# One core, cross-attention and soft mixture of experts: the first group's dispatch split into single batches

## The chip, the cores and the metric

The kernel runs on one core of a Trainium2 chip. A core has a matrix engine (PE), whose results go to the accumulator memory PSUM; a vector engine (DVE); a scalar engine for activation functions and copies (ACT); a general engine (POOL); and a queue that issues most transfers (SP). Each engine works through its own list of instructions in the order of the program, and semaphores make one engine wait for another. A matmul has two records: the load of the stationary 128 x 128 operand (PEld) and the pass of the moving columns over it (PE). Both are float32 here, and the trace has two passes for each matmul of the program. The metric is the device time of one execution in microseconds (us); a lower time is better.

## The reference, cut to what matters

There are 16 batches of 100 tokens with 256 features. Each batch attends to its own 361 context rows with 16 heads; then a soft mixture of 16 experts with 64 slots each runs on the normalized result.

```python
x = x + attention(layernorm(x), ctx_1024, ...)          # 16 heads of 16
z = layernorm(layernorm(x)) * norm_g + norm_b           # (b, n, d)
logits = einsum('bnd,esd->bnes', z, se)                 # 1024 slots
dispatch = softmax(logits, axis=tokens)
combine = softmax(logits, axis=slots)
slots = einsum('bnd,bnes->besd', z, dispatch)
gate = gelu(slots @ Wg + bg);  up = slots @ Wu + bu
eout = (gate * up) @ Wd + bd
x = x + einsum('bns,bso->bno', combine, eout)
```

The dispatch of a batch turns its 100 normalized tokens into 1024 slot vectors. Each expert needs its 64 slots of every batch of a group before it can start on that group.

## The kernel before, in words

**Groups and streams.** The batches go in five groups of 2, 2, 4, 4 and 4 (`GROUPS`). For each group there is a stream of attention units (`units`, four units to a batch, each with `maxima`, `queries`, `exponentials` and `values`), and then the dispatch in quarters of 256 slots (`dispatch_quarter`, four experts to a quarter) for each pair of batches. One stream, `all_experts`, runs the experts group by group: `gp` and `up` are the two first products (lines 1265 to 1281), `dn` the product with `Wd` (line 1225), `po` the combination (line 1147). While one group's experts run, the next group's attention is worked in between.

**The planner.** No engine order is written out by hand. At build time, `Clock` keeps a modelled time of each engine, every generator (`Task`) yields the earliest time of its next step, the PSUM banks that it takes and a triple of costs for PE, DVE and ACT, and the loop at the end of the kernel picks the next step. Before the first expert has run (`begun` is false), the steps that something waits for come first (`lead`: the units of the first group; after these `out_work`, the first entry of `dispatches` and `all_experts`). Another step is taken only if its modelled PE, DVE and ACT ends come no later than the next lead step's start plus a slack of 0.15 plus 0.6 of the step's PE cost. If nothing fits, PE gets a `warm_up` matmul on a constant (line 1319), which computes nothing that is used. After `begun`, units and dispatches go first, then side work from `fill` in the order of that list, and the experts fill what is left. While the first group's units run, the side work is sorted by a list of kinds.

**Around the change.** `out_work(b)` closes the attention of batch b: four divisions by the softmax sums on DVE (lines 699 to 707), the projection `o_ps` (line 712), the residual (line 720), the norm (lines 436 to 447), the normalized tokens `xn` (line 733), their transpose `xn_t` (line 738) and the scaled transpose `xnT` (line 744), with which `out_t[b]` is set. A quarter of the first group's dispatch then takes: the logits `lg` of both batches (line 928; 4 matmuls, 8 records, of 200 moving columns each), their maximum over tokens on DVE (line 953), four exponentials with sums on ACT (line 958), a copy of the logits to `lg_all` (line 949), the division on DVE (lines 980 and 983), four transposes `d_t` (line 1006), their copy `disp` (line 1011), the slots `sl` of each batch (line 1018), and the scaled slots, by DVE for the first batch (line 1030) and by ACT for the second (line 1033). At last the running maximum over slots, `top`, is kept up (lines 1050 to 1054), from which `combine_weights` starts. `slots_left[g, q]` counts how many parts of a quarter are outstanding; the experts of quarter q are gated on it.

Side work that can stand in the gaps before the first expert is `later_queries(2)` (`x_t` and `q_ps` of batches 2 and 3), `later_keys(2)` and `later_keys(3)` (context transposes `c_t`, keys `k_ps` on line 609, values `v_ps` on line 659).

**Queues.** SP issues the weights, the context rows (lines 199 to 213), the inputs and, for each batch's keys, four small copies of the mask row from `mrow_d` into `kT` (line 649). All of these share one queue in program order.

## Time and profile before

| | |
|---|---|
| median of 3 executions | 1183.79 us (1183.12 to 1184.21) |
| the profiled execution | 1184.91 us, its span 1183.0 us |
| PE busy | 1160.9 us, 98% of the span |
| ACT, DVE, POOL busy | 547.2, 632.9, 151.3 us |
| warm-up matmuls, line 1319 | 96 records from 1.4 to 78.7 us, 50 of them between 64 and 82 us |
| first expert matmul | 82.1 us |
| mean granted PE clock | 0.996 |

A span is the time from the first to the last recorded instruction; the execution's own time is about 2 us longer. "Busy" of PE counts warm-up matmuls too, so PE at 98% says nothing about how much of the first 82 us is of use. The timeline view gives the start, the length, the engine, the line and the tiles of merged instructions, and in brackets the idle time before them and who ended it.

### The profile page before, as it was taken

The numbers are of one execution on the slowest core, as the hardware profiler recorded it, in microseconds if no ns is written. First come the engines' busy times: TensorE is split into PE (matmuls) and PEld (weight loads), VectorE is DVE, ScalarE is ACT, GpSimd is POOL, SyncE is SP. The second block draws the span as 40 slices with busy tenths as digits, with TensorE's granted clock in tenths as the row PEclk, the third lists the DMA queues.
The fourth block names the chain that finished last, engine by engine and source line by source line (L and its number), as shares of the span: only waits on it lengthen the run. The fifth ranks groups of instructions, "written<-read, shape, count | busy, mean of one in ns | idle before, by whom it ended". The sixth has DMA issues, their size and how long they took to land.

```text
span 1183.0 us, 24384 instructions
## 1 busy us (share of the span) xinstructions
PE 1160.9 (98%) x9815; PEld 899.8 (76%) x9815; DVE 632.9 (53%) x1555; ACT 547.2 (46%) x1120; POOL 151.3 (13%) x255
## 2 busy tenths in 40 slices
PE   8899999999999999999999999999999999999998
PEld 6587878678788777667767777787878878777876
DVE  5755555475544566555386776656533455432222
ACT  3557554466454568444543745536312336314110
POOL 3110301013000043200010100024000003002000
PEclk9999999899999999999999999999999999999999
DMA  5413657345566613223341421333344343344441
GB/s 133 136 37 104 228 172 216 89 126 160 157 224 220 184 17 90 81 50 110 112 105 39 124 77 38 112 126 112 112 142 151 118 147 126 111 133 161 135 129 55
DMA packets 138675, 144.86 MB, mean 122 GB/s; under 512 B 45136, under 2 KB 97314, under 8 KB 138562
## 3 DMA queue, kind: packets, MB, share of 16 engines
q1 hardware_dynamic: 137742, 141.88, 39.5%
q8 instruction: 78, 1.28, 0.5%
q0 software_dynamic: 496, 1.12, 0.3%
q10 hardware_dynamic: 324, 0.29, 0.1%
q14 instruction: 35, 0.29, 0.1%
HBM read 141.60 MB, written 1.66 MB: 121 GB/s over the span
## 4 chain that ended last, share of the span: by engine, by line
PE 95%; DMA 2%; DVE 1%; SPq 1%; ACT 1%; issue 0%; DVEq 0%; ACTq 0%
PE dn L1225 19%; PE gp L1265 19%; PE up L1265 19%; PE sl L1018 5%; PE po L1147 5%; PE at L796 5%; PE at L771 4%; PE lg L928 4%; PE k_ps L609 3%; PE v_ps L659 3%; PE cx L819 3%; PE o_ps L712 1%; PE at L1319 1%; PE q_ps L538 1%; DMA kT<-mrow_d 1%; DVE mxp L776 1%
## 5 line engine op out<-in xcount | busy, mean ns | idle before, releaser
L1265 PE MATMUL gp<-ring,w_all 128*128 128x256 f32 (+1 forms) x1280 | 248.3, 341 | 1.5 <-ACT lg_all L949 1.3
L1265 PE MATMUL up<-ring,w_all 128*128 128x256 f32 (+1 forms) x1280 | 246.8, 340 | 0.0
L1281 DVE SCALAR_TENSOR_TENSOR hT<-up,parT,ge 128x256 f32<-128x256 f32 (+1 forms) x320 | 119.4, 423 | 225.0 <-PE up L1265 163.0
L1225 PE MATMUL dn<-w_all,hT 128*64 128x256 f32 x2048 | 232.8, 382 | 0.0
L1276 ACT ACTIVATE ge<-gp,parT 128x256 f32<-128x256 f32 (+1 forms) x320 | 117.2, 430 | 244.6 <-PE gp L1265 240.5
L1265 PEld LDWEIGHTS gp<-ring,w_all 128*128 128x128 f32 x1280 | 203.0, 191 | 28.5 <-issue 5.5
L1265 PEld LDWEIGHTS up<-ring,w_all 128*128 128x128 f32 x1280 | 203.5, 191 | 21.6 <-issue 1.7
L1225 PEld LDWEIGHTS dn<-w_all,hT 128*64 128x64 f32 x2048 | 143.8, 137 | 77.2 <-issue 10.1
L776 DVE TENSOR_REDUCE mxp<-at 100x4 f32<-100x1444 f32 x64 | 106.2, 1660 | 40.7 <-PE at L771 40.2
L1234 DVE TENSOR_TENSOR ring<-dn,bd_bc 128x512 f32<-128x512 f32 x64 | 44.3, 692 | 139.2 <-PE dn L1225 139.0
L804 ACT ACTIVATE aT<-at 121x1200 f32<-121x1200 f32 x64 | 74.9, 1171 | 55.2 <-PE at L796 49.5
L1276 ACT ACT_TABLE_LOAD x62 | 79.5, 1283 | 33.6 <-PE gp L1265 32.8
L998 DVE STREAM_TRANSPOSE disp<-d_ex 32x128 f32<-32x128 f32 x256 | 77.3, 302 | 4.6
L703 POOL TENSOR_TENSOR cxs<-cxs,rs 128x100 f32<-128x100 f32 x63 | 25.0, 398 | 410.4 <-DVE rs L700 328.6
L1033 ACT ACTIVATE ring<-sl,parT 128x256 f32<-128x256 f32 x64 | 32.7, 562 | 69.4 <-PE sl L1018 67.1
L1018 PE MATMUL sl<-disp,xn 100*128 100x256 f32 x256 | 62.6, 386 | 0.0
L1147 PE MATMUL po<-ring,lg_all 128*100 128x256 f32 x256 | 60.6, 383 | 0.2 <-DVE ring L1234 0.2
L983 POOL TENSOR_TENSOR d_ex<-d_ex,d_sm 128x400 f32<-128x400 f32 x28 | 23.9, 855 | 270.8 <-DVE d_sm L980 269.6
L796 PEld LDWEIGHTS at<-q,kT 32*121 32x121 f32 x1344 | 40.6, 180 | 19.9 <-issue 9.1
L771 PE MATMUL at<-kT,qp 32*100 32x361 f32 x448 | 49.2, 508 | 5.9 <-DMA kT<-mrow_d 5.9
L1018 PEld LDWEIGHTS sl<-disp,xn 100*128 100x128 f32 x256 | 46.6, 190 | 9.4 <-issue 2.8
L804 ACT ACT_TABLE_LOAD x35 | 44.9, 1283 | 18.4 <-PE at L796 10.3
(152 smaller groups left out, 1276.4 us busy)
## 6 DMA issues: line engine op xcount, KB each, us to landing
w_all<-in_L_ffn_Wg_dram SPq DMA_DIRECT2D x80, 512.0 KB
w_all<-in_L_ffn_Wu_dram SPq DMA_DIRECT2D x80, 512.0 KB
w_all<-in_L_ffn_Wd_dram SPq DMA_DIRECT2D x80, 512.0 KB
bd_bc<-in_L_ffn_bd_dram SPq DMA_DIRECT2D x80, 64.0 KB
c_sb<-in_ctx_dram SPq DMA_DIRECT2D x96, 44.0 KB
out_dram<-acc SPq DMA_DIRECT2D x8, 200.0 KB
acc<-in_x_dram SPq DMA_DIRECT2D x7, 200.0 KB
ring<-n_L_ffn_slot_embeds_dram POOLq DMA_DIRECT2D x1, 1024.0 KB, 7.2
```

What stands on the lines that cost most here:

```text
L771: nc.tensor.matmul(self.at[:N, r, :S2], lhsT=self.q[rows], rhs=self.k[rows], start=True, stop=True)
L776: nc.vector.tensor_reduce(mxv[:, :, m : m + 1], self.at[:N, :, :S2], AX.X, ALU.max, negate=True)
L796: nc.tensor.matmul(self.at[: KC + 1, r, c * N : (c + 1) * N], lhsT=self.k[rows, c * KC : c * KC + KC + 1], rhs=self.q2[rows], start=True, ...
L804: nc.scalar.activation(self.aT[: KC + 1], self.at[: KC + 1, :, : 3 * N], AF.Exp)
L928: nc.tensor.matmul(lg[:, c * 2 * N : (c + 1) * 2 * N], lhsT=seT[:, kd, (2 * q + c) * P : (2 * q + c + 1) * P], rhs=xnTs[g][:, kd, b0 * N : ...
L998: nc.vector.transpose(dst[toks, :, :, a, :], src[32 * a : 32 * a + 32, :, :, toks])
L1018: nc.tensor.matmul(sl[:, kd * 256 : (kd + 1) * 256], lhsT=xns[g][:, b0 + i, kd * P : (kd + 1) * P], rhs=disp[:, i, :], start=True, stop=True,)
L1147: nc.tensor.matmul(pos[i][:N, :D], lhsT=lg_all[:, slot, 2 * c + i, :], rhs=eouts_of(g, q)[:, c, 2 * p + i, :], start=c == 0, stop=c == 1,)
L1225: nc.tensor.matmul(dn[S * x : S * x + S, i * D : (i + 1) * D], lhsT=hts[x][fc // FB][0].rearrange("p (f b s) -> p f b s", f=FB, s=S)[:, fc ...
L1265: nc.tensor.matmul(ps[:, f * T : (f + 1) * T], lhsT=w[:, kd, fc * P : (fc + 1) * P], rhs=slots_of(g, q)[:, j, kd].rearrange("p b s -> p (b ...
L1276: nc.scalar.activation(ge[:, cols], ps[:, cols], AF.Gelu, bias=col(8, e, fc))
L1281: nc.vector.scalar_tensor_tensor(out=hT[:, cols], in0=ps[:, cols], scalar=col(NPAR, e, fc), in1=ge[:, cols], op0=ALU.add, op1=ALU.mult,)
```

## The change

The first group (batches 0 and 1) no longer goes through `dispatch_quarter`. A new generator, `dispatch_half(q, i)`, does one quarter for one batch: 100 moving columns in `lg`, two exponentials, two transposes, the slots of one batch with one half scaled on DVE and the other on ACT, and the running maximum of that batch. Batch 0's four quarters run one after the other in a new side task, `early_dispatch`, whose kind stands ahead of `key_work` in the sorted list and which is appended to `fill` ahead of `later_queries` and `later_keys`. Batch 1's four go into `dispatches`, where the four `dispatch_quarter` tasks stood. The counters `left` and `slots_left` of group 0 count batches in place of pairs. The other groups are as before.

```diff
+    half_slots, top_begun = {}, [False, False]
+    def dispatch_half(q, i):
+        def gate():
+            if i not in out_t or (q not in half_slots and not lg_free):
+                return NEVER
+            return max(seT_t[q // 2], out_t[i])
+        yield gate, 1, (0.9, 0.35, 0.75)
+        lg = mm_tile("lg")
+        for c in range(2):
+            for kd in range(KD):
+                nc.tensor.matmul(
+                    lg[:, c * N : (c + 1) * N],
+                    lhsT=seT[:, kd, (2 * q + c) * P : (2 * q + c + 1) * P],
+                    rhs=xnTs[0][:, kd, i * N : (i + 1) * N],
...
+        lgs = lg_all[:, half_slots[q]].rearrange("p (c i) n -> p i c n", i=2)[:, i]
...
+        ex = exs[:, :2, :N]
+        nc.vector.tensor_reduce(mx[:, :2], lgv, AX.X, ALU.max, negate=True)
+        for c in range(2):
+            nc.scalar.activation(ex[:, c], lgv[:, c], AF.Exp,
...
+        nc.scalar.copy(lgs, lgv)
...
+        yield t, 0, (0.0, 0.5, 0.0)
+        nc.vector.reciprocal(sm[:, :2], sm[:, :2])
+        nc.vector.tensor_tensor(ex, ex, sm[:, :2].unsqueeze(2).to_broadcast([P, 2, N]), ALU.mult)
+        yield t, 1, (0.25, 0.0, 0.4)
...
+        for c in range(2):
+            nc.tensor.transpose(tp[:N, c * P : (c + 1) * P], ex[:, c, :], ident)
+        nc.scalar.copy(disp, tp[:N, :256])
+        yield t, 1, (0.87, 0.4, 0.4)
+        sl = mm_tile("sl")
+        for kd in range(KD):
+            nc.tensor.matmul(
+                sl[:, kd * 256 : (kd + 1) * 256],
+                lhsT=xns[0][:, i, kd * P : (kd + 1) * P],
+                rhs=disp,
...
+            if kd == 0:
+                nc.vector.tensor_scalar(dst, srcv, ng_c[kd], nb_c[kd], ALU.mult, ALU.add)
+            else:
+                nc.scalar.activation(dst, srcv, AF.Identity, bias=nb_c[kd], scale=ng_c[kd])
...
+        slots_left[0, q] -= 1
+        left[0] -= 1
+        yield tl, 0, (0.0, 0.4, 0.0)
+        dst = top[0][:, i]
+        if not top_begun[i]:
+            nc.vector.tensor_tensor(dst, lgs[:, 0], lgs[:, 1], ALU.max)
+        else:
+            for c in range(2):
+                nc.vector.tensor_tensor(dst, dst, lgs[:, c], ALU.max)
+        top[1] += 0.5
+    def early_dispatch():
+        for q in range(NQ):
+            yield from dispatch_half(q, 0)
...
-    left = [n // 2 * NQ for n in GROUPS]
-    slots_left = {(g, q): n // 2 for g, n in enumerate(GROUPS) for q in range(NQ)}
+    left = [(n // 2 if g else n) * NQ for g, n in enumerate(GROUPS)]
+    slots_left = {(g, q): n // 2 if g else n for g, n in enumerate(GROUPS) for q in range(NQ)}
...
                     fill.append(Task(slot_work(), ck))
+                    fill.append(Task(early_dispatch(), ck))
                     load_x(1)
...
                     "out_work",
+                    "early_dispatch",
                     "key_work",
...
-                                dispatches.append(Task(dispatch_quarter(g, p, q), ck, 2))
+                                if g == 0:
+                                    dispatches.append(Task(dispatch_half(q, 1), ck, 2))
+                                else:
+                                    dispatches.append(Task(dispatch_quarter(g, p, q), ck, 2))
```

More of the change, by code (lines that the diff above doesn't have):

```diff
@@ L1057, in dispatch_quarter @@
         logits[g, p, q] = slot
+    half_slots, top_begun = {}, [False, False]
[12 more added lines that the diff above has]
+                    rhs=xnTs[0][:, kd, i * N : (i + 1) * N],
+                    start=kd == 0,
+                    stop=kd == KD - 1,
+                )
+        t = ck.run("PE", 0.85, ck.bank())
+        lgv = lg[:, : 2 * N].rearrange("p (c n) -> p c n", n=N)
+        if q not in half_slots:
+            half_slots[q] = lg_free.pop(0)
+            logits[0, 0, q] = half_slots[q]
+        lgs = lg_all[:, half_slots[q]].rearrange("p (c i) n -> p i c n", i=2)[:, i]
+        mx = two.tile([P, 4], F32, tag="mx", name="d_mx")
+        sm = two.tile([P, 4], F32, tag="sm", name="d_sm")
+        if len(exps) < 2:
+            exps.append(const.tile([P, 4, P], F32, name=f"d_ex{len(exps)}"))
+            nc.gpsimd.memset(exps[-1][:, :, N:], 0.0)
+        exs = exps[turn[0] % 2]
+        turn[0] += 1
+        ex = exs[:, :2, :N]
+        nc.vector.tensor_reduce(mx[:, :2], lgv, AX.X, ALU.max, negate=True)
+        t = ck.run("DVE", 0.35, t)
+        for c in range(2):
+            nc.scalar.activation(
+                ex[:, c],
+                lgv[:, c],
+                AF.Exp,
+                bias=mx[:, c : c + 1],
+                accum_out=sm[:, c : c + 1],
+            )
+            t = ck.act("exp", 130, t)
+        nc.scalar.copy(lgs, lgv)
+        tl = ck.copy(200, 0.0)
+        ck.free(tl)
+        yield t, 0, (0.0, 0.5, 0.0)
+        nc.vector.reciprocal(sm[:, :2], sm[:, :2])
+        ck.run("DVE", 0.1, t)
+        nc.vector.tensor_tensor(ex, ex, sm[:, :2].unsqueeze(2).to_broadcast([P, 2, N]), ALU.mult)
+        t = ck.run("DVE", 0.35)
+        yield t, 1, (0.25, 0.0, 0.4)
+        disp_sb = two.tile([P, 2, 256], F32, tag="disp", name="disp")
+        disp = disp_sb[:N, 0]
+        tp = mm_tile("d_t")
+        for c in range(2):
+            nc.tensor.transpose(tp[:N, c * P : (c + 1) * P], ex[:, c, :], ident)
+        nc.scalar.copy(disp, tp[:N, :256])
+        t = ck.copy(256, ck.run("PE", 0.25, t, ck.bank()))
+        ck.free(t)
+        yield t, 1, (0.87, 0.4, 0.4)
[5 more added lines that the diff above has]
+                rhs=disp,
+                start=True,
+                stop=True,
+            )
+        t = ck.pe(512, t, ck.bank())
+        ts = []
+        for kd in range(KD):
+            dst = slots_of(0, q)[:, :, kd, i, :]
+            srcv = sl[:, kd * 256 : (kd + 1) * 256].rearrange("p (e s) -> p e s", s=S)
+            if kd == 0:
+                nc.vector.tensor_scalar(dst, srcv, ng_c[kd], nb_c[kd], ALU.mult, ALU.add)
+                ts.append(ck.psum_dve(256, t))
+            else:
+                nc.scalar.activation(dst, srcv, AF.Identity, bias=nb_c[kd], scale=ng_c[kd])
+                ts.append(ck.copy(256, t))
+        ck.free(max(ts))
+        slot_t[0, q] = max(slot_t.get((0, q), 0.0), *ts)
+        slots_left[0, q] -= 1
+        left[0] -= 1
+        yield tl, 0, (0.0, 0.4, 0.0)
+        if (0, 0) not in tops:
+            tops[0, 0] = [two.tile([P, 2, N], F32, tag="top", name="top"), 0, 0.0]
+        top = tops[0, 0]
+        dst = top[0][:, i]
+        if not top_begun[i]:
+            nc.vector.tensor_tensor(dst, lgs[:, 0], lgs[:, 1], ALU.max)
+            top_begun[i] = True
+        else:
+            for c in range(2):
+                nc.vector.tensor_tensor(dst, dst, lgs[:, c], ALU.max)
+        top[2] = ck.run("DVE", 0.4, tl)
+        top[1] += 0.5
```

## The prediction

> **What bounds the kernel now.** I read the engine slices first, then busy time in windows.

> ```profile
> PE   8899999999999999999999999999999999999998
> 60.00:70.00 10.00, 9.48 (x95) 7.42 (x95) 7.58 (x25) 3.65 (x7) 1.45 (x4) 1.00 0.20 51
> 70.00:80.00 10.00, 9.99 (x68) 8.93 (x67) 4.71 (x13) 5.03 (x16) 2.68 (x5) 1.00 0.01 3
> 80.00:90.00 10.00, 9.02 (x65) 8.66 (x63) 3.56 (x8) 8.01 (x26) 0.00 (x0) 1.00 0.21 58
> ```

> PE is the bound from the first expert matmul (82.1 us) to the end; almost every window after 130 us is full. PE work added after 82 us therefore costs its length, and work moved from there into idle time before 82 us gains its length. Between 64 and 82 us PE looks full but is not: 50 of its records are warm-ups. At the chain's spacing (12 in 1.34 us, so 0.112 us each) that is 5.6 us without use.

> **When does the early half become possible?** This decides most. The timeline:

> ```profile
> 61.27 0.89 PE L796 MATMUL at<-q,kT 32*121 32x100 f32 x24 [0.35 <-DVE q L787]
> 63.77 0.72 PE L819 MATMUL cx<-aT,vpad 120*32 120x100 f32 x24
> 64.86 0.76 ACT L744 ACTIVATE xnT<-xn_t,parT 128x100 f32<-128x100 f32 x2
> 66.12 1.50 PE L1319 MATMUL at<-ident 128*128 128x128 f32 x12
> 68.77 1.38 PE L609 MATMUL k_ps<-cT,wk 128*128 128x361 f32 x4
> 69.98 1.89 PE L659 MATMUL v_ps<-wv,cT 128*121 128x256 f32 x8
> 72.96 1.52 PE L928 MATMUL lg<-xnT,seT 128*128 128x200 f32 x8
> 74.31 2.62 PE L1319 MATMUL at<-ident 128*128 128x128 f32 x22
> 78.95 1.99 PE L1018 MATMUL sl<-disp,xn 100*128 100x256 f32 x8
> ```

> The second batch's last unit is over at 63.77 (`cx`), and the first batch's `xnT` lands at 65.6. Its `out_work` has been low-priority DVE work since 44 us. So batch 0's quarters do not run during the second batch's units; there is nothing to dispatch until they are over. What remains is 65.6 to 73.0 us, while batch 1 goes through `out_work`, and the gaps of its first quarter up to 82 us. No lead step moves ahead of 64 us: the new task has no step ready, and key work of batch 1 stays within the eight side tasks that the planner looks at.

> **Part 1, PE work added.** `lg` had 8 records of 200 columns per quarter and gets 2 x 8 of 100 columns, each with its own load of 128 x 128. The chain of waits has both forms:

> ```profile
> 22.73 1.06 PE q_ps L538 x8
> 80.95 1.37 PE lg L928 x8
> ```

> Eight records of 100 columns take 1.06 us here, 0.97 from the first record to the next product (22.66 to 23.63), and 0.87 in another place (9.66). A halved column count thus does not halve the time; the load sets it. Per quarter 2 x 0.97 - 1.37 = 0.57 us; with the warm-up's load spacing, 2 x 8 x 0.112 - 1.37 = 0.42. Over four quarters +1.7 to +2.3, taken +2.0 us. `d_t` and `sl` keep their number and form.

> [...] The trace has 171 and 121 ns. [...] I use the row, +2.0.

> **Part 2, what the gaps take.** In `fill`, early dispatch stands ahead of the later queries and keys, so where a PE gap is long enough for one step it takes it from them. The k_ps at 68.77 (1.22 us by the chain) is where the first early `lg` goes: the planner sees some 1.9 us to the next lead step, and the step's triple (0.9, 0.35, 0.75) fits. Once its maxima and exponentials are on DVE and ACT, the key steps' own ACT cost no longer fits, so the gap's rest stays warm-up. I followed the planner's rule by hand with its costs and the trace's order:

> - lg, d_t and sl of quarter 0, batch 0 get in before the first expert, little more. Quarters 1 to 3 of batch 0 follow one another serially and must wait.
> - Displaced past the first expert: one k_ps (1.22), three v_ps (1.73 + 0.88), the x_t of batches 2 and 3 (about 0.5): 4.3 us.
> - Warm-ups stay at about 24 calls against 25: the chain of single steps that causes them is still there.

> **Part 3, the chain to the first expert gets shorter.** From `xnT` (73.04) to `gp` (82.14) it is 9.1 us. Batch 1 alone: lg -0.40; maximum over 200 and not 400 elements, 0.58 to about 0.36 (the 200-wide `top` takes 0.35): -0.22; two exponentials of 0.35 in place of four: -0.70; division -0.25; two transposes fewer -0.2; `disp` 0.59 to 0.37 (the 256-wide v_ps copy): -0.22; four sl records fewer -0.86; scaled slots split over DVE and ACT, one each: about -0.5; the next `lg` -0.40. Sum -3.8; the planner's own costs give -4.3. I take the first expert at 78 us, 4.0 earlier.

> **Part 4, after the first expert.** Dispatch work left on PE by then: before, 2.3 (rest of quarter 1) + 2 x 3.7 = 9.7 us; after, half of quarter 1 without its lg (1.2) and five whole halves of about 2.13 (0.97 + 0.3 + 0.86) = 11.8 us, +2.1. With the displaced 4.3 and the 4.0 gained: **+2.4 us** on PE.

> ACT is the other side. Exponential and gelu alternate here:

> ```profile
> 84.77 1.28 ACT L1276 ACT_TABLE_LOAD   x1
> 87.22 1.28 ACT L958 ACT_TABLE_LOAD   x1
> ```

> PE already waits once at 90.36 for PSUM that ACT frees late (1.35 us, the idle in window 80 to 90). Five half batches remain where two quarters did, so I expect one or two more pairs of loads (2.6 us each), and a half's fixed parts cost ACT about 0.25 us a quarter more (copies 2 x 0.3 + 2 x 0.37 against 0.50 + 0.59, two slot evictions unchanged). ACT was busy 22.7 of the 30 us from 80 to 110; plus 3 to 6 it is nearly full. [...] here ACT ended a copy at 84.74 and loaded at 84.77, so 1.28 stands. [...] Bounds of the PE stall: -1.35 (the stall there goes) to +4; nearest row is the one stall of 1.35, so I take **+0.9**.

> Three halves can be in flight over two `d_ex` buffers, so an exponential may wait for the transposes of the half two turns before. Queued behind it on ACT are gelu and the PSUM copies; cover is that those transposes are 0.3 us and picked first. Zero to +1, taken 0. DVE gets about 0.8 us more per quarter and is busy 36 to 78% of these windows: nothing. POOL's clearing of `d_ex` (0.32) only comes earlier, in idle POOL time. The change issues no DMA; the displaced keys' mask copies go out later, needed by batch 3's units after 110 us: nothing.

> **Sum.** +2.4 + 0.9 = +3.3 us on a span of 1183.0, so an execution of about 1188.2 against the profiled 1184.91. That one lay 1.1 us above the median; from 1183.79 the forecast is **1187 us**.

> **A lever that I cannot size.** The order after 82 us changes, and one stall later is large:

> ```profile
> 204.76 2.30 SPq L649 DMA_DIRECT2D kT<-mrow_d  x4
> 209.91 1.54 PE L771 MATMUL at<-kT,qp 32*100 32x361 f32 x8 [5.20 <-DMA kT<-mrow_d]
> 206.00:208.00 2.00, 0.00 (x0) 0.00 (x0) 0.00 (x0) 0.00 (x0) 0.00 (x0) 0.95 1.04 363
> 208.00:210.00 2.00, 0.09 (x4) 0.12 (x4) 0.00 (x0) 0.00 (x0) 0.00 (x0) 0.50 0.55 128
> ```

> Group 2's first unit waits for mask rows that SP could only issue behind batch 5's context loads and two weights. PE's granted clock falls to 0.50 and is 0.54 from 210 to 215. The stall costs 5.2 us and the slow clock some 2.5 to 3. Key work, context loads and unit follow each other as before, so I expect the stall to stay; but if the planner puts one more expert half (1.8 to 3.7 us) in front of the unit, or one less, it moves by that much.

> **Rivals.**
> - *The gaps are filled* (0.13). The 5.6 us of warm-ups take the early halves without displacing keys, and the 1.35 us stall goes: -5.6 - 1.35 + 2.0 = -5, 1179 us. For: 24 records' worth of gap lies in 74 to 82, where three early halves would fit by length. Against: each step must also fit by ACT, which the lead half holds. It decides if two or more whole early halves come before the first expert.
> - *Shorter stall at 205* (0.12). One more expert step before group 2's first unit: up to -7 with the clock fall gone, netting about 1180. Nothing in the profile favours it over its opposite.
> - *Longer stall there, or ACT the bound after 78 us* (0.25): +3 to +8 on top, 1190 to 1195.
> - *A wash* (0.12): the earlier first expert pays for displaced work and for half the loads, 1183 to 1185.
> - The forecast, *displaced, not hidden* (0.38): 1185.5 to 1189.

> **How the numbers follow.** About 0.2% (2.4 us) is what can be told from no change. Faster: most of the first two, 0.21. Same: the wash and the forecast's lower edge, 0.16. Slower: 0.63. Range 1179 to 1196: it takes in both lower rivals' centres and the longer stall; beyond lie about 0.2.

> **What would show it.** Right: `lg` of group 0 has 64 records near 0.12 us spacing; the first sits after 65 us; first `gp` near 78; k_ps, v_ps of batch 3 after it; warm-up records about 94 in all; a stall near 200 with a clock fall. Wrong: warm-ups down to 70 or fewer, an `lg` before 63 us, a first `gp` after 81, more than 2 us of new PE idle between 78 and 110, or a stall near 200 that is gone.

## The result, and the profile after

The changed kernel takes **1187.78 us** (median of 6 executions, 1187.06 to 1190.05); the kernel before took 1184.0 us beside it (6 executions, 1183.12 to 1185.81). The ratio is 1.0034, 95% interval 1.0021 to 1.0047: slower by about a third of a per cent. The profiled execution took 1187.36 us with a span of 1185.6 us, against 1184.91 and 1183.0.

First the engine slices and the windows of the changed kernel (in the windows: the stretch, its length, the busy time and number of instructions of PE, PE's weight loads, DVE, ACT and POOL, the granted clock, the DMA share, GB/s).

```profile
PE   8899999999999899999999999999999999999998
60.00:70.00 10.00, 9.64 (x104) 8.22 (x105) 7.56 (x25) 3.79 (x8) 1.82 (x4) 1.00 0.17 49
70.00:80.00 10.00, 9.57 (x73) 8.71 (x72) 4.08 (x13) 5.93 (x22) 0.33 (x3) 1.00 0.01 2
80.00:90.00 10.00, 8.18 (x50) 6.40 (x50) 6.60 (x18) 7.59 (x25) 1.97 (x2) 1.00 0.19 54
```

The third window is the one to look at: PE is busy 8.18 us where it was busy 9.02. PE's idle time here has grown from 0.98 to 1.82 us, and ACT, which the prediction suspected, is busy 7.59 and was busy 8.01. In the slices of the whole span a dip has appeared too, the 8 in the fourteenth slice, at about 400 us.

The timeline of the changed kernel, cut to what answers the prediction:

```profile
63.39 0.72 PE L819 MATMUL cx<-aT,vpad 120*32 120x100 f32 x24
68.39 1.03 PE L1073 MATMUL lg<-xnT,seT 128*128 128x100 f32 x8
69.26 1.75 PE L1425 MATMUL at<-ident 128*128 128x128 f32 x14
...
77.73 2.36 PE L1371 MATMUL gp<-ring,w_all 128*128 128x128 f32 x16
81.88 1.48 PE L609 MATMUL k_ps<-cT,wk 128*128 128x361 f32 x4
84.17 1.13 PE L659 MATMUL v_ps<-wv,cT 128*121 128x256 f32 x4 [0.81 <-ACT lg_all L1105]
85.36 1.27 POOL L563 TENSOR_TENSOR acc<-acc,bo_bc 100x512 f32<-100x512 f32 x1 [0.85 <-DVE d_sm L1109]
85.39 1.46 DVE L1111 TENSOR_TENSOR d_ex<-d_ex,d_sm 128x200 f32<-128x200 f32 x1
87.00 0.40 PE L1118 MATMUL d_t<-ident,d_ex 128*100 128x128 f32 x2 [0.84 <-DVE d_ex L1111]
```

The second batch's units end at 63.39 and the first early `lg` comes at 68.39. Nothing of batch 0's dispatch lies beside those units. The first expert is at 77.73, 4.4 us earlier by the trace's own time, 4.0 if both traces are set to the first `xn_t` of batch 0 (64.4 and 64.0 us). The `k_ps` and `v_ps` that used to stand at 68.77 and 69.98 now stand behind it. Warm-ups are 94 records, before 96.

The stall at 205 us is gone. The plan now has an expert's `dn`, the `q_ps` and eight `k_ps` records between the issue of the mask rows and the unit that needs them, which starts 9.3 us after that issue (before, it started 5.2 us after it, and PE was idle all that time):

```profile
207.00 2.31 SPq L649 DMA_DIRECT2D kT<-mrow_d  x4
208.74 3.67 PE L1331 MATMUL dn<-w_all,hT 128*64 128x256 f32 x32
216.32 0.87 PE L771 MATMUL at<-kT,qp 32*100 32x361 f32 x8
```

In its place stands a stall near 400 us. Windows of the changed kernel around both places, and its timeline at the second:

```profile
206.00:208.00 2.00, 2.00 (x11) 1.66 (x10) 0.00 (x0) 1.24 (x4) 0.00 (x0) 1.00 0.32 50
400.00:402.00 2.00, 0.00 (x0) 0.00 (x0) 1.93 (x6) 0.33 (x2) 0.70 (x1) 1.00 0.01 5
404.00:406.00 2.00, 2.00 (x8) 1.58 (x7) 1.28 (x3) 0.59 (x1) 0.00 (x1) 0.50 0.33 94
```

```profile
400.18 0.87 DVE L1264 SCALAR_TENSOR_TENSOR acc<-po,c_sm,acc 100x256 f32<-100x256 f32 x2
...
400.96 0.91 DVE L594 STREAM_TRANSPOSE cT<-c_sb 128x704 f32<-128x704 f32 x1
401.90 0.25 DVE L595 STREAM_TRANSPOSE cT<-c_sb 128x64 f32<-128x64 f32 x1
402.07 0.14 DVE L980 RECIPROCAL d_sm<-d_sm 128x4 f32<-128x4 f32 x1
...
402.30 1.68 PE L609 MATMUL k_ps<-cT,wk 128*128 128x361 f32 x4 [3.66 <-DVE d_sm L980]
```

PE stands still for 3.66 us for `k_ps`. The list names `d_sm`, which ended last, but what `k_ps` reads is `cT`, transposed on DVE until 402.15 behind a row of norm and residual work. In the kernel before the same stretch looks like this:

```profile
395.92 3.67 PE L1225 MATMUL dn<-w_all,hT 128*64 128x256 f32 x32
```

There one expert's `dn` stood between the same `lg` and the DVE list, and covered it. The plan of the changed kernel has that `dn` at 389.26, ahead of the `lg`.

Where the time went, counted on PE from the first `xn_t` to the last `dn` (1109.8 us before, 1111.7 after):

| part | us |
|---|---|
| `lg` records, their spacing summed, first `xn_t` to group 2 | 22.5 to 24.2, +1.7 |
| PE idle, 64 to 110 us | 1.35 to 2.43, +1.1 |
| waits too short to show as idle, the same stretch (record spacing over the usual one of its kind) | about +0.4 |
| stall at 205 us with its half clock (6.8 us) gone | -6.6 |
| stall at 402 us with its half clock (3.4 us) new | +6.1 |
| idle between 443 and 778 us | 1.80 to 1.13, -0.7 |

That is +2.0 for a measured +1.9. The two rows of the stalls are sums of record spacing over the usual one and can be off by about half a microsecond. Two places check the table, because both kernels have done the same work on PE there but for the 32 added `lg` records and two warm-ups. At the 145th `gp` record (159 us) the changed kernel is 3.8 us behind, counted from `xn_t`; at the 513th (443 us) it is 2.65 behind. After 406 us the order of PE's records is the same in both.

The profiled pair differs by 2.45 us and the medians by 3.8, so the table explains the traces and not the whole of the medians' difference. Outside this stretch the traces of all kernels here scatter: the first `xn_t` comes between 64.0 and 73.6 us (52.4 in the run that moves the tokens forward), and 8.4 to 9.8 us pass from the start of the last `dn` to the end. So distances from the first `xn_t` to the last `dn` are given below beside the medians.

### The profile page after: what moved, and what is told of

It reads as the page before. It is cut to its first block, busy times and chain, and to the rows that moved or that the text cites. A ratio compares the mean times of both kernels' runs of the same rounds, so it can differ in the third digit from the quotient of the medians.

```text
span 1185.6 us, 24470 instructions
## 1 busy us (share of the span) xinstructions
PE 1163.6 (98%) x9845; PEld 901.5 (76%) x9845; DVE 635.7 (54%) x1572; ACT 551.4 (47%) x1132; POOL 151.3 (13%) x255
## 3 DMA queue, kind: packets, MB, share of 16 engines
q8 instruction: 78, 1.28, 0.5%
## 4 chain that ended last, share of the span: by engine, by line
PE 94%; DVE 2%; issue 1%; ACT 1%; DMA 1%; POOL 0%; SPq 0%; DVEq 0%; ACTq 0%; POOLq 0%
PE dn L1331 19%; PE up L1371 19%; PE gp L1371 19%; PE po L1253 5%; PE at L796 4%; PE sl L1018 4%; PE at L771 4%; PE k_ps L609 3%; PE lg L928 3%; PE cx L819 3%; PE v_ps L659 3%; PE o_ps L712 1%; PE q_ps L538 1%; DVE mxp L776 1%; PE at L785 1%
## 5 line engine op out<-in xcount | busy, mean ns | idle before, releaser
L1033 ACT ACTIVATE ring<-sl,parT 128x256 f32<-128x256 f32 x56 | 28.6, 561 | 59.9 <-PE sl L1018 59.9
L1018 PE MATMUL sl<-disp,xn 100*128 100x256 f32 x224 | 55.0, 388 | 0.7 <-ACT disp L1011 0.7
L796 PEld LDWEIGHTS at<-q,kT 32*121 32x121 f32 x1344 | 40.6, 180 | 19.1 <-issue 8.2
L796 PE MATMUL at<-q,kT 32*121 32x100 f32 x1344 | 49.9, 277 | 3.4 <-DVE q L787 3.3
L700 DVE RECIPROCAL rs<-rs 128x100 f32<-128x100 f32 x64 | 49.8, 778 | 2.2
```

Of the source, the lines that this page charges most:

```text
L700: nc.vector.reciprocal(rs, rs)
L796: nc.tensor.matmul(self.at[: KC + 1, r, c * N : (c + 1) * N], lhsT=self.k[rows, c * KC : c * KC + KC + 1], rhs=self.q2[rows], start=True, ...
L1018: nc.tensor.matmul(sl[:, kd * 256 : (kd + 1) * 256], lhsT=xns[g][:, b0 + i, kd * P : (kd + 1) * P], rhs=disp[:, i, :], start=True, stop=True,)
```

## Experiments

Two things were open: which part of the change costs (the loads, the early task, or merely another plan), and whether the stalls at 205 and 402 us belong to the change or are an accident of the plan.

**The doubled loads alone.** In the kernel before, the first group's `lg` is cut in two halves of 100 columns; costs and plan stay as they are.

```diff
+        parts = 1 if g else 2
+        w = 2 * N // parts
         for c in range(2):
-            for kd in range(KD):
+            for h in range(parts):
+                for kd in range(KD):
...
```

> The kernel before, with each 200-column logits matmul of the first group cut into two of 100 columns; the plan and the order of all else are unchanged. Theory (the load of the stationary operand sets the time of a 100-column record): the 64 records take about 0.11 to 0.12 us each where 32 took 0.17, so +1.4 to +2.3 us, about 1185.9 beside 1184.0, and the first expert matmul about 0.8 us later. Rival (moving columns alone set the time): no change, within 0.5 us.

Measured: 1185.33 us against 1185.07 beside it, ratio 1.0005 (0.9995 to 1.0016). From `xn_t` to the last `dn` 1110.7, +0.9; the `lg` records themselves take 1.7 to 1.8 us more and the first expert is 0.8 us later. So the doubled records are real work on PE: 100 columns don't take half of 200. In the trace before, eight 128 x 128 loads took 1.40 us beside 200 columns (72.77 us), and 0.97 beside 100 (22.66 us) as beside 128 (warm-ups, 20.23 us). With PE's order unchanged, 1.25 us of them are left at 101 us, and a shorter wait between 600 and 650 us takes off another 0.5. The total was less than expected, and its interval includes no change.

**Single batches, all from the list of dispatches.** Both batches go through `dispatch_half`, and there is no side task.

```diff
-                    fill.append(Task(early_dispatch(), ck))
...
                                 if g == 0:
+                                    dispatches.append(Task(dispatch_half(q, 0), ck, 2))
                                     dispatches.append(Task(dispatch_half(q, 1), ck, 2))
```

> The changed kernel without its early task: both batches of the first group go singly through the list of dispatches, after the second batch's tokens are ready. Theory (the early halves only displaced key and value work): the keys and values of batch 3 go back in front of the first expert, the first expert matmul comes at 79 to 82 us, and at the 128th gate record after it (about 119 us) the kernel stands within 1.5 us of the changed one; total 1185 to 1189. Rival (the early halves fill idle time): 3 us or more behind the changed kernel at that place, total above 1190.

Measured: 1186.3 us, ratio 1.0006 (0.9995 to 1.0016); `xn_t` to the last `dn` 1110.2, +0.4. The edit does not do what was expected of it: batch 0 does not wait for batch 1's tokens. The first entry of `dispatches` is a lead step, and of the tokens its gate asks for batch 0's alone. So two `lg` of batch 0 stand ahead of batch 1's `xn_t`, the last line here:

```profile
66.48 0.39 PE L738 MATMUL xn_t<-ident,xn 100*128 100x100 f32 x2
67.40 1.23 PE L1073 MATMUL lg<-xnT,seT 128*128 128x100 f32 x8
...
73.54 1.03 PE L1073 MATMUL lg<-xnT,seT 128*128 128x100 f32 x8
...
75.36 0.39 PE L738 MATMUL xn_t<-ident,xn 100*128 100x100 f32 x2
```

The first comes 0.9 us after the first `xn_t`; in the changed kernel it was 4.3. This run, and the two below that have the same edit, thus compare batch 0 in the lead with batch 0 in the side list, not a late dispatch with an early one. Batch 1's tokens pay for it: their `xn_t` comes 8.9 us after the first, where it was 7.4 before and 6.8 with the change.

The first expert comes 16.6 us after `xn_t` (17.7 before, 13.7 with the change), with 86 warm-ups. From 171 us on PE's order is the one of the kernel before; there the run is 1.7 us behind, and shorter waits later leave 0.4 (the stall at 205 us is there again, now 4.5 us, with a half clock of 6.8 us). The side list thus brings 2.9 us of the earlier first expert, and the end of the kernel does not see it: the change is 1.5 us behind this run by the trace, and about 3.3 by the ratios.

**The early task behind the keys.** `early_dispatch` is appended to `fill` after `later_keys(3)`.

```diff
-                    fill.append(Task(early_dispatch(), ck))
                     load_x(1)
...
                     fill.append(Task(later_keys(3), ck))
+                    fill.append(Task(early_dispatch(), ck))
```

> The changed kernel with the early task put behind the later queries and keys in the side list. Theory (one gap step is traded for another): k_ps and v_ps come back before the first expert, the early logits move behind them, the first expert matmul comes at 80 to 84 us, and warm-ups stay at 85 to 100 records; total within 2 us of the changed kernel unless a later stall moves. Rival (the order of the side list is what costs): warm-ups fall below 75 records and the total falls by 3 us or more against the changed kernel, to 1184 or less.

Measured: 1191.46 us, ratio 1.0063 (1.0042 to 1.0084); `xn_t` to the last `dn` 1115.8. The first expert does not come at 80 to 84 us but here:

```profile
L1371 PE MATMUL gp<-ring,w_all x77: 275/275/377, 100.8 to 130.0; 128*128 128x128 f32 x77
```

(The tile view: count, shortest, median and longest ns, first and last start.) Warm-ups go up to 170 records, 126 of them after 60 us. The idea that keys would fill the gaps first and batch 0 come just after was wrong. Once batch 1's dispatch is a lead step, a task at the end of the list starves: four `lg` start from 72.8 to 88.2 us, after batch 1's tokens, and a fifth at 94.5, just before the first expert, which needs both batches. The gaps are then filled with matmuls that compute nothing. The end of the list is no place for the early task.

**Batch 0's tokens earlier.** In the list of kinds, `out_work` goes ahead of `slot_work` (which prepares the slot vectors that `lg` needs).

```diff
-                    "slot_work",
                     "out_work",
+                    "slot_work",
                     "early_dispatch",
```

> The changed kernel with out_work ahead of the parameter and slot work in the sorted list of side work, so that the first batch's tokens are ready before the second batch's last unit. Theory (DVE has no room for both before the units end: whichever comes second, tokens or slot vectors, keeps the logits late): xnT of batch 0 lands near 50 to 54 us, seT only at 65 to 70 us, the first logits matmul still not before 63 us, total 1186 to 1192. Rival (only the order kept the early halves out of the units): first logits before 60 us, warm-ups down to 75 records or fewer, first expert matmul before 76 us and a total of 1182 to 1185.

Measured: 1190.75 us, ratio 1.0044 (1.0029 to 1.0059). The first `xn_t` comes at 52.4 us, 11.6 us earlier, yet the slot vectors `seT` land only at 70.3 us, the first `lg` is at 71.4, the first expert at 97.6, and there are 148 warm-ups. As expected, whichever of the two inputs of `lg` is second keeps it after the units. In neither order does an early half stand beside the second batch's units.

**The stall at 205 us: mask rows first.** In the kernel before, from batch 4 on the context loads of the next batch go out behind the mask rows of this one. The same edit in the changed kernel, and in the kernel with single batches.

```diff
-        if b + 1 < B and b + 1 not in loads:
+        if b < 4 and b + 1 < B and b + 1 not in loads:
             load_kv(b + 1)
...
+        if b >= 4 and b + 1 < B and b + 1 not in loads:
+            load_kv(b + 1)
```

> The kernel before, with the next batch's context load issued on SP after the mask rows of this batch's keys instead of before them (batches 4 and later). Theory (SP's order makes the stall at 205 us): the 5.2 us wait for the mask rows goes, and with it the 6.8 us at half clock, which costs 3.4: up to -8.6, total 1176 to 1179. Rival (the rows land late because the transfer engines are busy, or another input of the same unit is as late): less than 2 us is gained.

> The changed kernel with the mask rows of the keys issued on SP ahead of the next context load, as in e4. Theory (the changed kernel has lost the stall at 205 us already, and its own stall near 399 us comes from DVE's list, not from SP): little is gained by the queue itself, total 1183 to 1188, behind e4 by 3 us or more. Rival (both stalls come from SP's order): the stall near 399 us goes as well, total 1179 to 1182, level with e4 but for the 1 to 2 us of doubled loads.

> e2 (both batches singly, none early) with the mask rows first, as in e4. Theory (doubled loads cost 1 to 2 us, the early task costs another 2 to 3): 1181 to 1183 where e4 had 1180.1, and 2 us or more ahead of e5. Rival (the loads are hidden and the early task costs nothing; stalls make all of the difference): within 0.7 us of e4, or level with e5.

Measured: before 1180.12 us, ratio 0.9956 (0.9944 to 0.9967), 1104.8 us from `xn_t` to the last `dn`, no stall over 1.4 us and no half clock at 205. With the change 1192.17, ratio 1.0052 (1.0037 to 1.0067), 1114.7, above both expectations, with a wait of 3.66 us before a `k_ps` at 405.8 us and one of 2.04 at 431.6. With single batches 1183.17, ratio 0.9981 (0.9974 to 0.9989), 1106.0. So the old form does have 5 us to gain at 205 (8.6 were thought possible), from the order of the queue alone. Single batches, again with batch 0 in the lead, cost 1.7 us in this plan by 170 us, where PE's order becomes the same, and 1.2 at the end (`lg` +1.9, warm-ups -0.65), close to what the loads are worth; by the ratios it is 3. The change itself landed on the worse side: it never had the stall at 205, and the edit left it its other one. Which of the later waits make up its further 3 us is open.

**A plan without either stall.** The planner's own assumption of how long after its issue a mask row can be used, `MASK_DMA`, goes from 5 to 9 and to 12 us. In the trace before, the first `kT` copies of these keys (line 630) ended at 197.79 us and the unit that needs their mask rows began at 209.91, 12.1 us later. The edit adds no work that is used. It changes the order, and with it what depends on the order: warm-ups (96 become 112 and 158 in the kernel before, 94 become 86 and 124 in the changed one), some ACT table loads, and which engine makes some copies.

```diff
-MASK_DMA = 5.0
+MASK_DMA = 9.0
```

> The kernel before with the planner's allowance for the mask rows' landing at 9 us in place of 5; nothing else is edited, but the plan after the first group moves. Theory (the 205 us stall is the planner's 5 us against some 12 us on the chip): group 2's first unit stands some 4 us later in PE's list, 4 of the 5.2 us of stall and the half clock after it go: 1177 to 1181. Rival (the stall moves with the plan): 1183 or more.

> The changed kernel with the same allowance of 9 us. Theory (the change costs 1 to 2 us of doubled loads and about 3 us by the early task, and has no mask stall to lose): 1184 to 1191, 3 us or more behind the kernel before with 9 us. Rival (the change costs its loads alone): 1 to 2.3 us behind it.

> The kernel before with an allowance of 12 us. Theory: no mask stall and no half clock at 205 us, 1176 to 1182; a unit that waits longer in the plan can cost elsewhere. Rival: 1183 or more.

> The changed kernel with an allowance of 12 us. Theory: 3 us or more behind the kernel before with 12 us, unless a stall of its own plan comes or goes; the first expert matmul stays 3 to 5 us ahead of that kernel's. Rival: 1 to 2.3 us behind it.

| planned distance | before, us | changed, us | `xn_t` to last `dn` | medians' difference |
|---|---|---|---|---|
| 5 us (as given) | 1184.0 | 1187.78 | 1109.8, 1111.7 | +3.8 |
| 9 us | 1177.46, ratio 0.9946 (0.9926 to 0.9966) | 1181.27, 0.9983 (0.9974 to 0.9991) | 1100.9, 1104.6 | +3.8 |
| 12 us | 1189.63, 1.005 (1.0035 to 1.0065) | 1192.4, 1.007 (1.0053 to 1.0086) | 1106.8, 1108.1 | +2.8 |

(Ratios are against the kernel before at 5 us. At 9 us the intervals of the two forms lie apart; at 12 us they overlap.) With 12 us the kernel *before* has the stall that looked like the change's own. From the list of waits of that run:

```profile
PE k_ps L609 <- DVE d_sm L980: 3.7, 1, 3.7
```

It is the same 3.7 us before a `k_ps`, at 405 us, and a fall of the clock follows, 6.8 us long. So this stall belongs to a plan in which no expert's `dn` stands there, not to the change.

At 9 us neither kernel has a stall over 1.5 us after 66 us, nor a half clock before its end, and the change costs 3.8 us by medians and 3.7 by the trace. This pair is clean of the two large stalls. The waits of PE from 60 to 300 us, first before, then changed (total, times, longest):

```profile
PE at L771 <- DMA kT<-mrow_d: 1.1, 1, 1.1
```

```profile
PE k_ps L609 <- DVE cT L595: 1.4, 1, 1.4
PE d_t L1118 <- ACT d_ex L1097: 1.4, 1, 1.4
```

From `xn_t` to the first `gp` of group 2 it is 370.8 us before and 374.6 changed, +3.8: `lg` +1.3, idle +2.3, warm-ups -2.7, and +2.9 spread over `dn`, `gp`, `sl`, `k_ps`, `d_t` in waits shorter than a record. Some 2.6 us of it are there by 177 us; the rest comes with the wait of 1.4 us for `cT` at 194 us. Here more of the gaps was used (86 warm-ups against 112, and the first expert 2.4 us nearer to `xn_t`), and it still did not pay.

**The clean plan with batch 0 in the lead.** The edit of the single batches, at 9 us. Here too an `lg` of batch 0 stands 2.2 us after the first `xn_t`, and a second one before batch 1's tokens.

> This is the pair of kernels in which neither stall at 205 us nor the one at 400 us occurs (planned mask distance 9 us), with the change's smaller half alone: both batches of group 0 go one by one through the new function, but none of it is side work ahead of the keys. The old form took 1177.46 us at this distance, the whole change 1181.27. Theory (two prices of about equal size: the doubled lg loads, and the early task's displaced key work and short waits): 1178.5 to 1180.0 us, 1.0 to 2.5 behind the old form, first gp near 83 us, lg +1.3 to +1.8 us in the records. Rival (the loads are the whole price, the early task is free): level with the whole change, 1180.8 to 1182. Second rival (the early task is the whole price): level with the old form, 1177 to 1178. A stall near 205 or 400 us with a clock fall would make the run useless for this.

Measured: 1181.29 us, ratio 0.9967 (0.9959 to 0.9975); `xn_t` to the last `dn` 1104.2. By the ratio it lies halfway between the old form and the change at this distance; by the trace it is 3.4 us behind the old form and only 0.4 ahead of the change. It has 90 warm-ups, so 22 of the 26 that the change saves here come without the side task. The theory's 1178.5 to 1180 was missed. But the loads are not the whole price either: `lg` is only +1.2. Its wait list from 66 to 440 us begins

```profile
PE k_ps L609 <- DVE cT L595: 1.4, 1, 1.4
```

which is the wait at 194.9 us that the changed kernel has at 194.5 and the old form has not. It arises from the plan that single batches lead to, with batch 0 in either place. The side list moves the first expert from 19.2 to 16.6 us after `xn_t` and gives back all of the 2.6 us and 0.4 more.

## Why the prediction was right, and where it was not

**The total.** 1187 was forecast and 1187.78 measured. The size of the sum, +3.3, is also what the stretch it was made for shows: +1.7, +1.1 and +0.4 make +3.2 us by about 75 us after `xn_t`. The pair at 9 us has +3.7, 2.6 of it by 177 us. But between that stretch and the end two stalls changed places, which the forecast did not see, and their near balance (-6.6, +6.1) is luck of this plan. That the total lies so near the forecast rests on this balance too.

**When the half becomes possible: right.** First `lg` at 68.39, not before 65, and none beside the second batch's units. The run with the tokens moved forward adds what the forecast lacked: the slot vectors are then as late.

**Part 1, loads: right in kind, a little large.** Taken +2.0, measured +1.7 in the changed kernel, 1.7 to 1.8 alone, +1.2 to +2.2 in the other runs. The row of the trace that it was taken from, 0.97 us for eight records of 100 columns against 1.37 for eight of 200, was a good guide. On the path it can be less: alone the loads cost only 0.9 at the end.

**Part 2, displaced and not hidden: right.** 94 warm-ups as forecast; ahead of the first `gp` stand 4 `k_ps`, 12 `v_ps` and 4 `x_t` records fewer, about 4.2 us at their usual spacing, where 4.3 was forecast; `k_ps` at 81.88 and `v_ps` at 84.17 stand behind the first `gp`. Of the three `lg` that come before it (68.39, 71.82, 76.86) the second is batch 1's, since the slots ready at 75.89 are what the first `gp` needs; so batch 0 gets quarter 0 and at most one `lg` more, "little more" as forecast. In the plan with 9 us 26 warm-ups were saved, which is on the way to the forecast's first rival, and the change still cost 3.7 us. That rival's price was wrong too: it took warm-ups saved for time saved.

**Part 3, first expert 4.0 earlier: right**, 4.0 us. From batch 1's `lg` to `gp` it is 5.9 us where it was 9.2, so 3.3 us come from the chain, for which the forecast had 3.8; the rest is that this `lg` starts earlier, 7.8 us after `xn_t` where it was 8.5. With batch 0 in the lead only 1.1 us are gained.

**Part 4: the term that was wrong in kind.** The forecast took +0.9 us of PE stall from one or two more pairs of ACT table loads. The changed kernel has five table loads between 64 and 110 us (79.38, 81.84, 98.66, 102.28, 105.32); the kernel before had five (84.77, 87.22, 92.30, 97.73, 103.44). There is no extra pair (up to 130 us it is nine against nine), and ACT is less busy from 82 to 92 us than before (6.75 us against 8.44). The stall of 1.35 us for a PSUM bank is shorter, 0.8, and in place of the rest PE waits for the half's own chain: `d_t` for the division on DVE (1.0 us in two waits), `d_t` for the scaled slots on ACT (0.3) and `sl` for `disp` on ACT (0.2). The size came out close, +1.1, but from another engine: PE's waits on ACT add up to 1.4 us, as before, and the growth is the 1.0 us on DVE. The step that failed is "DVE gets about 0.8 us more per quarter and is busy 36 to 78% of these windows: nothing". Its mean load said nothing on one division that met POOL's addition (1.46 us in place of 0.37) and on which `d_t` waited. That a serial chain of half-size steps also has more places to wait is an argument; no run isolates it.

**The stall at 205: wrong.** "I expect the stall to stay" failed; the forecast had named its absence as a sign against it. It is gone because the plan puts other work there. The forecast's lever, one expert step more or less in front of a unit, is what happened, at 205 in one direction and at 402 in the other. The rival "shorter stall" counted only the first of these. That such stalls move freely, and aren't the change's, is shown by the 12 us plan of the kernel before.

**What stays open.** What batch 0's place costs, and what dispatching it early costs at all. Between the lead and the side list it is 0.4 us by the trace in the plan with 9 us, where both kernels share one order after 171 us, and 1.9 by the ratios; with 5 us it is 1.5 and 3.3, though other stalls lie between them. No run holds batch 0 back until batch 1's tokens are ready, so the price of an early half beside a late one is not measured.

## What to carry to other kernels

Work that starts an engine's bound stretch earlier gains only what it takes out of idle time; here a first expert 4 us earlier was paid back by displaced keys, by loads that did not shrink with the columns (eight in 0.97 us beside 100 columns as beside 128), and by waits in the new chain. When a planner sets the order, any edit moves stalls of several microseconds far from its place, so compare two forms in more than one plan before you believe a third of a per cent. And look at those stalls themselves first: telling the planner that mask rows take 9 us and not 5 made the kernel before 1177.46 us, more than anything else tried here. It is no rule, though: with 12 us the same kernel took 1189.63.

## What the runs showed of the hardware

**A DVE operation beside a POOL operation took four times as long.** The division of 200 elements took 1.46 us at 85.39 beside POOL's addition (85.36 to 86.63), and 0.37 us elsewhere. It ended 0.22 us after POOL's end. In the kernel before, the 400-wide division at 76.78 met the same addition and took 0.73 against 0.57 to 0.58. In the run with the early task behind the keys the two met at another time, with a later start of the division, and it ended 0.22 us after POOL again:

```profile
75.01 1.27 POOL L563 TENSOR_TENSOR acc<-acc,bo_bc 100x512 f32<-100x512 f32 x1 [1.01 <-DVE z L504]
75.32 1.19 DVE L1111 TENSOR_TENSOR d_ex<-d_ex,d_sm 128x200 f32<-128x200 f32 x1
```

In all 14 traces together, 149 DVE operations took clearly longer than is usual for them (by over 15% and 0.04 us), and each of the 149 overlapped one of POOL and ended after it, by a time that is the same for all of one form to 0.01 us. In the kernel before these are nine, in the changed one eleven: 0.15 us after POOL's end for 100x256 on lines 504 and 733, 0.12 for 128x100 on line 707, 0.22 for 128x200, 0.43 for the division of 400. Why DVE takes longer there is not shown by any run; the forecast had not reckoned with it.

```profile
399.99:403.40 3.41, 1.10 (x4) 0.79 (x5) 3.34 (x11) 0.34 (x2) 1.82 (x3) 1.00 0.22 60
403.40:406.81 3.41, 3.41 (x12) 2.46 (x11) 2.12 (x4) 0.59 (x1) 0.60 (x1) 0.50 0.43 112
...
400.53:403.94 3.41, 1.65 (x8) 0.98 (x6) 2.79 (x10) 3.35 (x17) 0.44 (x2) 1.00 0.21 78
403.94:407.36 3.42, 1.52 (x7) 1.03 (x8) 3.39 (x9) 0.00 (x0) 2.19 (x3) 1.00 0.22 60
```

In the changed kernel 2.31 us of idle PE fall into one piece, and the next is at half clock. With mask rows first a border splits the gap into 1.76 and 1.90 us, and nothing follows. From 60 to 1160 us of all 14 traces this holds throughout: the clock fell after each of the six pieces with 2.31 us of idle or more (3.08 in the kernel before, 2.31 in the changed one), and after none with 1.90 or less. It stayed at half for a second piece where the first still had 1.2 to 2.1 us of idle (four cases), and came back where the first had none (two cases, and all four second pieces). Between 1.90 and 2.31 us no run has a case, and before 60 us idle time alone does not decide it: the clock fell there after pieces with 1.07 and 1.24 us and not after one with 1.47.
